# Routed experts in units of four, two and one blocks: 120, 16 and 20 of them where 85, 64 and 64 were

## The chip, the core and the metric

The kernel runs on one core of a Trainium2 chip. The metric is device time in microseconds (us) of one execution, the median of the runs shown. Engines are named as in the profile: PE (TensorE, with PEld for its weight loads), DVE (VectorE), ACT (ScalarE), POOL (GpSimd), SP (SyncE, which here only issues DMAs).

## What is computed

An input of 8 x 1024 rows of 512 goes through a modulated linear layer and then through a mixture of experts whose result is added to the input. Cut to what matters:

```python
y = clip(((x * styles) @ weight.T) * dcoefs + bias, -256, 256)   # per batch row
shared = silu(y @ sh_gate_w) * (y @ sh_up_w) @ sh_down_w          # hidden 1024
topk_idx, w = _route(y, router_w, e_bias)                         # 8 of 64 experts a row, by groups
order = argsort(topk_idx.reshape(-1), stable=True)                # rows sorted by expert
g, u = ragged_dot(sorted_x, gate_w, sizes), ragged_dot(sorted_x, up_w, sizes)   # hidden 256
o = ragged_dot(silu(g) * u, down_w, sizes) * weight_of_row
out = x + shared + zeros.at[tok].add(o)
```

There are 8192 x 8 = 65,536 pairs of a row and an expert. The expert biases are spread widely, so the lists of the experts are of very unequal length, from none to 8191 rows.

## The kernel before, in words

**Precision.** Every product is made of three matmuls in the fast fp32 form: the operand is split into a rounded part ("hi", written by ACT) and a rest ("lo", written by DVE), and hi x hi, hi x lo and lo x hi are summed in PSUM.

**Stages.** First the modulated layer writes its rows y to DRAM (L316 to L373). Then a shared stage of 16 x 8 = 128 steps computes the shared expert (L1100 to L1161). Beside it a generator, `route_slots` (L814), sorts the rows by expert: it is driven a little at a time from each step; its small matmuls (`later`) run in the next step, and each `HOP` ends its turn for one step. It writes 512 columns of (row, weight) to a DRAM table by indirect DMAs, five a step (L1031), reads the table back in groups of 128 blocks (L1000), holds it until step 119 (L1154), and turns it into `slot_tok` and `slot_w` (L1006). The last four steps also begin the first routed unit (`early`).

**Blocks and units.** A block is 128 rows of one expert. The number of blocks of an expert, in binary, gives its fours, at most one two and at most one one. The places of the blocks are numbered ones first, then twos, then fours, each aligned to its size. A static list of units (L777 to L787) covers these places: units of one, two and four blocks, with 4 x NU = 532 blocks. Since the places are aligned, a unit of one can also do a quarter of a four, or a half of a two. Which expert a unit belongs to is computed on the chip (`iexp`, L949). Fours beyond the 133 places of four go to tail units behind the list, groups of 8, 4, 2 and 1 under branches (L1173 to L1179).

**A unit** (`plan`, L608). Each block is gathered by an indirect DMA of POOL into `xg` (12 buffers, L534), turned by four PE transposes (L538) and split into `xh` and `xl` (two buffers, by the unit's parity). The expert's weights are loaded by SP (L531) into a raw buffer, `wg` for gate and up and `wd` for down; the load is skipped when the buffer already holds this expert. ACT and DVE split them (L549, L69) into `gh`, `gl`, `dh`, `dl` (two buffers, by parity), which for unit i may begin only when unit i-2 has ended its gate and up. There are three raw buffers: one for the ones, one for the fours, one for the twos.

Gate and up of a four or a two (`part`, L561) have the weights as the loaded operand and all rows of the unit as the moving one: 48 matmuls of 512 columns for a four, of 256 for a two. A one (`half`, L570) has the rows as the loaded operand and gate and up together as 512 moving columns: 12 matmuls, after which the hidden row block must be turned by two transposes (L575). The hidden rows are split too (`hh`, `hl`); `down_c` (L581) runs six matmuls of 512 columns for each block, ACT scales the result by the row's weight (L585), and POOL adds it into the output with an accumulating indirect DMA (L588). The first such DMA of a unit waits until all of the unit before have landed.

**The order of the work.** `plan` gives each task an engine, a duration, a delay, the tasks it depends on and a due time. `arrange` (L729) runs through them in model time: an engine that is free takes, of its tasks that are ready, the one due first. The order that comes out is the program order on PE, ACT, DVE, SP and POOL. `DOWN` and `TURN` (L605, L606) set by how much, for each size of unit, the downs come after the hidden rows and the turns ahead of gate and up (first number), and the distance from block to block (second number).

Of the kernel before, what the change touches and what calls it, by code (L numbers as in the profile page):

```python
# [13 lines left out]
I32 = mybir.dt.int32  # L14
# [7 lines left out]
P = 128  # L22
# [8 lines left out]
KC = C // P  # L31
HC = HS // P
QT = 512
NH = E
NP = E
NF = 85
NU = NF + NH // 4 + NP // 2
TBITS = 4
GROUPS = [(b, 1 << b) for b in range(TBITS - 1, -1, -1)]
NX = (1 << TBITS) - 1  # L40
NSB = (NU + NX) * 4
NE = NH + NP + NF + NX
NTRASH = 4 * P
# [20 lines left out]
def body(ctx, tc, xT, x, condT, wT, vecs, affT, rwT, ebias, wexp, shgu, shdn, cst, out):  # L64
# [28 lines left out]
    tbit = pp.tile([P, 8], I32, name="tbit")  # L93


    dctx = ExitStack()
# [401 lines left out]
    class Unit:  # L498


        def __init__(self, unit, block, nb, i):
# [100 lines left out]

    DOWN = {1: (-8.5, 1.0), 2: (0.0, 4.2), 4: (3.4, 5.4)}  # L605
    TURN = {1: (9.9, 1.0), 2: (1.4, 3.4), 4: (16.6, 0.0)}  # L606

    def plan(units):  # L608

# [14 lines left out]
        for n, u in enumerate(units):  # L624
# [6 lines left out]
                before = [T[lw, x, 2 if a else c] for x in ("wh", "wl") for c in ((0, 1) if a == 0 else (2,))] if lw is not None else []  # L631
                add((i, "load", a), "SP", 0.1, 12.0 if a == 0 else 8.0, due - 22 + 4 * a, lambda u=u, a=a: load(u, a), *before)
            for c in range(2):
                add((i, "wh", c), "ACT", 1.08, 0.15, due - 4.8 + 2.2 * c, lambda u=u, c=c: w_hi(u, c), T[i, "load", 0], get((i - 2, "gu")))
                add((i, "wl", c), "DVE", 1.22, 0.15, due - 3.7 + 2.2 * c, lambda u=u, c=c: w_lo(u, c), T[i, "wh", c], get((i - 2, "gu")))
            xlo = []
            for s in range(u.nb):
                g = ng
# [74 lines left out]
                    lo.append(l_)  # L713
                ddue = t0 + 2.5
            for c in (2,):
                add((i, "wh", c), "ACT", 1.08, 0.15, ddue - 2.4, lambda u=u, c=c: w_hi(u, c), T[i, "load", 1], *hq)
                add((i, "wl", c), "DVE", 1.22, 0.15, ddue - 1.2, lambda u=u, c=c: w_lo(u, c), T[i, "wh", c], *hq)
# [61 lines left out]
    for i in range(sum(want)):  # L779
        lag = [want[k] * (i + 1) / sum(want) - count[k] for k in range(3)]  # L780
        kind = 2 if i == 0 else max((k for k in range(3) if count[k] < want[k] and not (k == 0 and units[-1].nb == 1)), key=lambda k: lag[k])
        n = count[kind]
        count[kind] += 1
        units.append((
            lambda: Unit(n, n, 1, i), lambda: Unit(NH + n, NH + 2 * n, 2, i), lambda: Unit(NH + NP + n, NH + 2 * NP + 4 * n, 4, i),
        )[kind]())
    assert tuple(count) == want  # L787
    tasks, byname = plan(units)
    groups, r = [], 0
    for b, size in GROUPS:  # L790
        groups.append((b, [Unit(NH + NP + NF + r + q, 4 * (NU + r + q), 4, q) for q in range(size)]))
        r += size

    with ExitStack() as bctx:
# [19 lines left out]
        def route_slots():  # L814
# [102 lines left out]
            V.tensor_scalar(tbit[:, TBITS:TBITS + 1], ti[:, 5:6], 1, None, ALU.min)  # L917
# [11 lines left out]
            V.tensor_scalar(g2[:, :TBITS], gp[:E, :TBITS], 4.0, 4.0 * NU, ALU.mult, ALU.add)  # L929
            off = 0  # L930
            for b, n in GROUPS:
                V.tensor_scalar(ex[:, off:off + n], cs[:E, C_GRP:C_GRP + n], g2[:, b:b + 1], None, ALU.add)
                off += n
            yield 1.8

# [29 lines left out]
            for g in range(0, NSB, P):  # L965
                n = min(P, NSB - g)

                bk = sbt.tile([E, 2, P], F32, name="bk")
                V.tensor_scalar(bk[:, 0], block[:E], float(g), None, ALU.add)
                m0 = 4 * NU - g  # L970
                if m0 < n:
                    V.tensor_copy(bk[:, 0, m0:n].rearrange("e (u f) -> e u f", f=4), ex.unsqueeze(2).to_broadcast([E, NX, 4]))
# [12 lines left out]
                later.append(row)  # L985
                yield HOP
# [18 lines left out]
                    n = min(P, NSB - g * P)  # L1005
                    PE.transpose(ps[:, q * P:q * P + n], tg[g][:n].rearrange("b (s w) -> b w s", w=2)[:, w], ident[:n, :n])  # L1006

            whole = NSB // P
            for part in ([(g, 0) for g in range(whole)], [(g, 1) for g in range(whole)], [(whole, 0), (whole, 1)]):
                later.append(lambda part=part: turn(part))  # L1010
                yield HOP
                if part[0][0] == 0:
                    V.tensor_copy((slot_tok, slot_w)[part[0][1]][:, :whole * P], ps[:, :whole * P])
                else:
                    for w in range(2):
                        V.tensor_copy((slot_tok, slot_w)[w][:, whole * P:], ps[:, w * P:w * P + NSB - whole * P])
            yield 0


# [68 lines left out]
        with tc.manual_schedule(engines={ET.PE, ET.SP, ET.Activation, ET.DVE}):  # L1088
# [11 lines left out]
            for i, (j, c) in enumerate(steps):  # L1100
# [66 lines left out]
    with cctx:  # L1167
        allot(cctx.enter_context(tc.tile_pool(name="cp", bufs=1, reuse_waits="tile")), kinds, None)
        allot(cctx.enter_context(tc.tile_pool(name="psc", bufs=1, space=PSUM, reuse_waits="tile")), pkinds, None)
        with tc.manual_schedule(engines={ET.PE, ET.SP, ET.Activation, ET.DVE}):  # L1170
            for t in arrange(tasks, begun):
                t.do()
            with tc.If(nc.values_load(tbit[0:1, TBITS:TBITS + 1], min_val=0, max_val=1) > 0):  # L1173
                for b, tail in groups:
                    held.clear()
                    line[0] = None
# [46 lines left out]
```

## Time and profile before

| | |
|---|---|
| median of 3 runs | 3764.27 us (3763.72 to 3764.33) |
| the profiled execution itself | 3764.38 us |
| its span, first to last instruction | 3762.5 us |
| mean granted clock of PE over the span | 0.995 |
| PE / DVE / ACT / POOL busy | 99% / 59% / 50% / 57% |
| routed stage, 1325 to 3742 us: PE busy | 2415.56 of 2417.00 us |
| moved by DMA | 467.79 MB, mean 124 GB/s |

The modulated layer takes the first two to three fortieths of the span, the shared stage lasts until about 1325 us, and the rest is the routed stage. Two kinds of lines are used below. A piece of the chain is a stretch of the chain of work that ended last: start, length, engine, tile, line and count; its length is the distance to the next piece, so that it can be added up. A window gives, for a stretch of the span, its length, then for each engine its busy time and count, then the granted clock, the busy share of the DMA engines and what they moved in GB/s. The busy time of a single matmul overlaps that of the next and can't be added up.

### The profile page before, as it was taken

To read this page: it belongs to the slowest core of one execution; us is meant where nothing else is said; L and a number is where in the kernel's file an instruction comes from. 1 tells how busy PE (TensorE), PEld (TensorE's weight loads), DVE (VectorE), ACT (ScalarE), POOL (GpSimd) and SP (SyncE) were. 2 spreads that over 40 slices of the span, in tenths; PEclk is the share of its full clock that TensorE was granted. 3 is DMA by queue.
4 is the path that set the end of the run, shared out by engine and by line. 5 is a ranking of instruction groups with operands and counts; after the bars stand their busy time and mean duration, and the time that the engine had idled before them with its cause. 6 is when DMAs were issued, how large, how long until landed. Compare 5 with 4: busy or idle time off the path is not lost.

```text
span 3762.5 us, 53389 instructions
## 1 busy us (share of the span) xinstructions
PE 3721.5 (99%) x19047; PEld 3120.3 (83%) x19047; DVE 2206.0 (59%) x3376; ACT 1888.8 (50%) x2891; POOL 2127.6 (57%) x1596
## 2 busy tenths in 40 slices
PE   9999999999999999999999999999999999999998
PEld 7777888888888888888888888888888888888886
DVE  6766656666542265666556566556566656656654
ACT  5652112111111166666666566666566666666664
POOL 0003666666654066666666565566665666666663
PEclk9999999999999999999999999999999999999999
DMA  7762212222122277787777776766766766666664
GB/s 252 234 175 65 66 35 52 52 48 55 38 49 58 95 185 168 157 210 168 168 162 152 157 148 137 152 131 137 165 126 125 136 133 117 135 115 116 118 116 65
DMA packets 234392, 467.79 MB, mean 124 GB/s; under 512 B 42578, under 2 KB 75362, under 8 KB 228355
## 3 DMA queue, kind: packets, MB, share of 16 engines
q0 software_dynamic: 135792, 280.15, 40.5%
q1 hardware_dynamic: 97331, 183.06, 15.8%
q8 instruction: 152, 2.49, 0.3%
q14 instruction: 125, 1.02, 0.1%
q10 hardware_dynamic: 992, 1.06, 0.1%
HBM read 532.75 MB, written 195.63 MB: 194 GB/s over the span
## 4 chain that ended last, share of the span: by engine, by line
PE 95%; DVE 2%; DMA 1%; ACT 1%; issue 0%; SPq 0%; POOL 0%; DVEq 0%; POOLq 0%; ACTq 0%
PE pg L561 35%; PE po L581 20%; PE gu L121 18%; PE po L1061 9%; PE pg L570 5%; PE pt L538 4%; PE py L316 3%; DMA xr<-in_xT 1%; PE pg L575 0%; PE plt L341 0%; DVE yl L69 0%; DVE yt L353 0%; DVE xl L300 0%; ACT yf L322 0%; DMA yr<-yT_d 0%
## 5 line engine op out<-in xcount | busy, mean ns | idle before, releaser
L588 POOL DMA_INDIRECT out<-oc,tokw x532 | 955.0, 1795 | 563.6 <-ACT oc L585 250.0
L534 POOL DMA_INDIRECT xg<-y_d,tokw x532 | 595.4, 1119 | 440.8 <-PE pt L538 194.4
L1031 POOL DMA_INDIRECT tab_d<-tokw,ad x512 | 564.8, 1103 | 492.7 <-DVE h L133 205.8
L561 PE MATMUL pg<-xh,gh 128*128 128x512 f32 (+1 forms) x2384 | 834.1, 350 | 0.0
L561 PE MATMUL pg<-xh,gl 128*128 128x512 f32 (+1 forms) x2384 | 823.5, 345 | 0.0
L561 PE MATMUL pg<-xl,gh 128*128 128x512 f32 (+1 forms) x2384 | 820.8, 344 | 0.0
L69 DVE TENSOR_TENSOR gl<-wg,gh 128x1024 fp32r<-128x1024 f32 x426 | 519.6, 1222 | 108.1 <-ACT gh L549 96.9
L561 PEld LDWEIGHTS pg<-xh,gl 128*128 128x128 f32 x2384 | 449.8, 189 | 57.1
L561 PEld LDWEIGHTS pg<-xl,gh 128*128 128x128 f32 x2384 | 449.9, 189 | 55.7
L561 PEld LDWEIGHTS pg<-xh,gh 128*128 128x128 f32 x2384 | 449.8, 189 | 53.0
L549 ACT CAST gh<-wg 128x1024 fp32r<-128x1024 f32 x426 | 448.2, 1055 | 0.0
L585 ACT ACTIVATE oc<-po,tokw 128x512 f32<-128x512 f32 x532 | 369.5, 695 | 153.1 <-PE po L581 136.2
L69 DVE TENSOR_TENSOR xl<-pt,xh 128x512 fp32r<-128x512 f32 x532 | 356.4, 686 | 137.0 <-ACT xh L541 106.4
L581 PE MATMUL po<-dh,hh 128*128 128x512 f32 x1064 | 427.0, 401 | 1.0 <-ACT hh L710 1.0
L581 PE MATMUL po<-dh,hl 128*128 128x512 f32 x1064 | 418.4, 393 | 0.4 <-DVE hl L69 0.4
L581 PE MATMUL po<-dl,hh 128*128 128x512 f32 x1064 | 416.0, 391 | 0.0
L121 PE MATMUL gu<-yh,guh 128*128 128x512 f32 x1024 | 401.7, 392 | 3.1 <-ACT yh L72 3.1
L121 PE MATMUL gu<-yl,guh 128*128 128x512 f32 x1024 | 403.1, 394 | 0.2 <-DVE yl L69 0.2
L708 DVE TENSOR_TENSOR hf<-hf,pg 128x512 f32<-128x512 f32 x170 | 116.8, 687 | 483.6 <-PE pg L561 473.7
L121 PE MATMUL gu<-yh,gul 128*128 128x512 f32 x1024 | 400.2, 391 | 0.0
L541 ACT CAST xh<-pt 128x512 fp32r<-128x512 f32 x532 | 301.2, 587 | 177.2 <-PE pt L538 81.6
L69 DVE TENSOR_TENSOR dl<-wd,dh 128x1024 fp32r<-128x1024 f32 x213 | 260.4, 1223 | 89.5 <-ACT dh L549 69.5
(234 smaller groups left out, 5615.2 us busy)
## 6 DMA issues: line engine op xcount, KB each, us to landing
wg<-in_wexp SPq DMA_DIRECT2D x213, 1024.0 KB
wd<-in_wexp SPq DMA_DIRECT2D x213, 512.0 KB
y_d<-yt SPq DMA_DIRECT2D x64, 256.0 KB
xn<-in_x SPq DMA_DIRECT2D x64, 256.0 KB
out<-xn SPq DMA_DIRECT2D x64, 256.0 KB
xr<-in_xT SPq DMA_DIRECT2D x60, 256.0 KB
yT_d<-yf SPq DMA_DIRECT2D x60, 256.0 KB
yr<-yT_d SPq DMA_DIRECT2D x60, 256.0 KB
```

Of the source, the lines that this page charges most:

```text
L69: V.tensor_tensor(o, a, b, ALU.subtract)
L121: i_ = PE.matmul(p_, lhsT=w_[:, q * KC + k], rhs=y_[k], start=n == 0, stop=n == 3 * KC - 1)
L534: queued(GP.indirect_dma_start(xg[g % RXG].bitcast(F32), None, y_d, IOA(slot_tok[:, u.block + s:u.block + s + 1], 0)))
L541: S.copy(xh[u.xq][:, :, s * P:(s + 1) * P], pt_of(g).bitcast(F32))
L549: S.copy(a[u.q][:, sl], (wg, wg, wd)[c][u.kind][:, sl])
L561: PE.matmul(out, lhsT=w_[u.q][:, c:c + P], rhs=x_[u.xq][:, k, :w], start=n == 0, stop=n == 3 * KC - 1)
L570: PE.matmul(out.rearrange("p (o h) -> p o h", o=2), lhsT=x_[u.xq][:, k, :P], rhs=wv[:, k], start=n == 0 and i == 0, stop=n == 5 and i == 1)
L581: PE.matmul(po[d % 2], lhsT=h_[u.q][:, k, s * P:(s + 1) * P], rhs=w_[u.q][:, k * C:(k + 1) * C], start=n == 0, stop=n == 5)
L585: S.mul(oc[d % ROC], po[d % 2], slot_w[:, u.block + s:u.block + s + 1])
L588: i_ = queued(GP.indirect_dma_start(out, IOA(slot_tok[:, u.block + s:u.block + s + 1], 0), oc[d % ROC], None, compute_op=ALU.add))
L1031: i_ = GP.indirect_dma_start(places, IOA(ad, 0), tw, None)
L1061: PE.matmul(acc[j][s], lhsT=h_[:, ts], rhs=w_[c], start=c == 0 and n == 0, stop=c == HC - 1 and n == 2)
```

## The change

The static list keeps 133 places of four, but covers them by 120 fours, 16 twos and 20 ones. Since there are now fewer ones and twos than experts, a surplus has to be taken care of: experts beyond the twentieth with a single block have it rounded up to a two, and those beyond the sixteenth with a two have it rounded up to a four (two more matmuls and two more turns of the generator). The rounding can push more fours over the 133 places, so the tail grows from 15 to 47 units: five groups of eight and groups of four, two and one. The table of slots grows from 592 to 720 blocks, six groups of 128 for five.

The raw weights of the fours go to two buffers in turn, and ones and twos share the third. The due times of the turns, the downs and the splits of the weights are others.

```diff
-NH = E
-NP = E
-NF = 85
+NH = 20
+NP = 16
+NF = 120
 NU = NF + NH // 4 + NP // 2
-TBITS = 4
-GROUPS = [(b, 1 << b) for b in range(TBITS - 1, -1, -1)]
-NX = (1 << TBITS) - 1
+TBITS, TBIG = 3, 5
+GROUPS = [(TBITS + q, 8) for q in range(TBIG)] + [(b, 1 << b) for b in range(TBITS - 1, -1, -1)]
+NX = sum(n for _, n in GROUPS)
+TANY = TBITS + TBIG
...
-            self.kind = {1: 0, 4: 1, 2: 2}[nb]
+            self.kind = 2 if nb < 4 else n % 2
...
-    DOWN = {1: (-8.5, 1.0), 2: (0.0, 4.2), 4: (3.4, 5.4)}
-    TURN = {1: (9.9, 1.0), 2: (1.4, 3.4), 4: (16.6, 0.0)}
+    DOWN = {1: (-8.2, 1.0), 2: (6.6, 5.1), 4: (6.6, 5.1)}
+    TURN = {1: (9.9, 1.0), 2: (13.2, 1.9), 4: (18.0, -1.3)}
...
-                add((i, "wh", c), "ACT", 1.08, 0.15, due - 4.8 + 2.2 * c, ...
-                add((i, "wl", c), "DVE", 1.22, 0.15, due - 3.7 + 2.2 * c, ...
+                add((i, "wh", c), "ACT", 1.08, 0.15, due - 8.3 + 2.2 * c, ...
+                add((i, "wl", c), "DVE", 1.22, 0.15, due - 7.2 + 2.2 * c, ...
...
-                add((i, "wh", c), "ACT", 1.08, 0.15, ddue - 2.4, ...
-                add((i, "wl", c), "DVE", 1.22, 0.15, ddue - 1.2, ...
+                add((i, "wh", c), "ACT", 1.08, 0.15, ddue + 3.8, ...
+                add((i, "wl", c), "DVE", 1.22, 0.15, ddue + 5.0, ...
...
             V.tensor_scalar(eci[:, 0:1], eci[:, 0:1], 7, None, ALU.logical_shift_right)
+            for most, bit in ((NH, 0), (NP, 1)):
+                V.tensor_scalar(eci[:, 1:2], eci[:, 0:1], bit, 1, ALU.logical_shift_right, ALU.bitwise_and)
+                V.tensor_copy(ecnt[:, 1:2], eci[:, 1:2])
+                later.append(lambda: PE.matmul(ps[:E, 1:2], lhsT=cs[:E, C_CUM:C_CUM + E], rhs=ecnt[:, 1:2], start=True, stop=True))
+                yield HOP
+                V.tensor_scalar(ecnt[:, 2:3], ps[:E, 1:2], most + 0.5, float(1 << bit), ALU.is_gt, ALU.mult)
+                V.tensor_tensor(ecnt[:, 2:3], ecnt[:, 2:3], ecnt[:, 1:2], ALU.mult)
+                V.tensor_copy(ecnt[:, 3:4], eci[:, 0:1])
+                V.tensor_tensor(ecnt[:, 3:4], ecnt[:, 3:4], ecnt[:, 2:3], ALU.add)
+                V.tensor_copy(eci[:, 0:1], ecnt[:, 3:4])
...
-            whole = NSB // P
-            for part in ([(g, 0) for g in range(whole)], [(g, 1) for g in range(whole)], [(whole, 0), (whole, 1)]):
+            half_ = [(g, w) for w in range(2) for g in range(4, NG)]
+            for part in ([(g, 0) for g in range(4)], [(g, 1) for g in range(4)], half_):
...
-                    for u in [units[next(q for q in range(len(units)) if units[q].kind == k)] for k in (1, 0)]:
+                    for u in [units[next(q for q in range(len(units)) if units[q].kind == k)] for k in (0, 1)]:
```

The other edits fit the tail's bits, the experts of its units and the copies out of the table to the new sizes. With these numbers the static list begins F F 1 F F 2 F F F (F a four, 1 a one, 2 a two) where it began F 1 2 F 1 2 F 1 2, has 156 units for 213, and ends with F F for 2 F.

More of the change, by code (lines that the diff above doesn't have):

```diff
@@ L92, in body @@
     iexp = pp.tile([1, NE], I32, name="iexp")
-    tbit = pp.tile([P, 8], I32, name="tbit")
+    tbit = pp.tile([P, TANY + 1], I32, name="tbit")
     dctx = ExitStack()
@@ L498, in body, with __init__ @@
     class Unit:
-        def __init__(self, unit, block, nb, i):
+        def __init__(self, unit, block, nb, i, n):
             self.unit, self.block, self.nb, self.i = unit, block, nb, i
-            self.kind = {1: 0, 4: 1, 2: 2}[nb]
+            self.kind = 2 if nb < 4 else n % 2
             self.q, self.xq, self.e = i % 2, i % RX, None
@@ L633, in plan @@
             for c in range(2):
-                add((i, "wh", c), "ACT", 1.08, 0.15, due - 4.8 + 2.2 * c, lambda u=u, c=c: w_hi(u, c), T[i, "load", 0], get((i - 2, "gu")))
-                add((i, "wl", c), "DVE", 1.22, 0.15, due - 3.7 + 2.2 * c, lambda u=u, c=c: w_lo(u, c), T[i, "wh", c], get((i - 2, "gu")))
+                add((i, "wh", c), "ACT", 1.08, 0.15, due - 8.3 + 2.2 * c, lambda u=u, c=c: w_hi(u, c), T[i, "load", 0], get((i - 2, "gu")))
+                add((i, "wl", c), "DVE", 1.22, 0.15, due - 7.2 + 2.2 * c, lambda u=u, c=c: w_lo(u, c), T[i, "wh", c], get((i - 2, "gu")))
             xlo = []
@@ L715, in plan @@
             for c in (2,):
-                add((i, "wh", c), "ACT", 1.08, 0.15, ddue - 2.4, lambda u=u, c=c: w_hi(u, c), T[i, "load", 1], *hq)
-                add((i, "wl", c), "DVE", 1.22, 0.15, ddue - 1.2, lambda u=u, c=c: w_lo(u, c), T[i, "wh", c], *hq)
+                add((i, "wh", c), "ACT", 1.08, 0.15, ddue + 3.8, lambda u=u, c=c: w_hi(u, c), T[i, "load", 1], *hq)
+                add((i, "wl", c), "DVE", 1.22, 0.15, ddue + 5.0, lambda u=u, c=c: w_lo(u, c), T[i, "wh", c], *hq)
             chain = [T[units[n - 1].i, "out", s] for s in range(units[n - 1].nb)] if n else []
@@ L784, in body @@
         units.append((
-            lambda: Unit(n, n, 1, i), lambda: Unit(NH + n, NH + 2 * n, 2, i), lambda: Unit(NH + NP + n, NH + 2 * NP + 4 * n, 4, i),
+            lambda: Unit(n, n, 1, i, n), lambda: Unit(NH + n, NH + 2 * n, 2, i, n), lambda: Unit(NH + NP + n, NH + 2 * NP + 4 * n, 4, i, n),
         )[kind]())
@@ L790, in body @@
     for b, size in GROUPS:
-        groups.append((b, [Unit(NH + NP + NF + r + q, 4 * (NU + r + q), 4, q) for q in range(size)]))
+        groups.append((b, [Unit(NH + NP + NF + r + q, 4 * (NU + r + q), 4, q, q) for q in range(size)]))
         r += size
@@ L916, in route_slots @@
             yield 1.8
-            V.tensor_scalar(tbit[:, TBITS:TBITS + 1], ti[:, 5:6], 1, None, ALU.min)
+            V.tensor_scalar(tbit[:, TANY:TANY + 1], ti[:, 5:6], 1, None, ALU.min)
+            for q in range(TBIG):
+                V.tensor_scalar(tbit[:, TBITS + q:TBITS + q + 1], ti[:, 5:6], float(-8 * q - 7), 0.0, ALU.add, ALU.max)
+            V.tensor_scalar(tbit[:, TBITS:TANY], tbit[:, TBITS:TANY], 1, None, ALU.min)
             for b in range(TBITS - 1, -1, -1):
@@ L931, in route_slots @@
             for b, n in GROUPS:
-                V.tensor_scalar(ex[:, off:off + n], cs[:E, C_GRP:C_GRP + n], g2[:, b:b + 1], None, ALU.add)
+                V.tensor_scalar(ex[:, off:off + n], cs[:E, C_GRP:C_GRP + n], g2[:, b:b + 1] if b < TBITS else 4.0 * (NU + off), None, ALU.add)
                 off += n
@@ L969, in route_slots @@
                 V.tensor_scalar(bk[:, 0], block[:E], float(g), None, ALU.add)
-                m0 = 4 * NU - g
+                m0 = max(4 * NU - g, 0)
                 if m0 < n:
-                    V.tensor_copy(bk[:, 0, m0:n].rearrange("e (u f) -> e u f", f=4), ex.unsqueeze(2).to_broadcast([E, NX, 4]))
+                    x0, xn_ = (g + m0) // 4 - NU, (n - m0) // 4
+                    V.tensor_copy(bk[:, 0, m0:n].rearrange("e (u f) -> e u f", f=4), ex[:, x0:x0 + xn_].unsqueeze(2).to_broadcast([E, xn_, 4]))
                     V.tensor_tensor(bk[:, 0, m0:n], bk[:, 0, m0:n], four[:E, m0:n], ALU.add)
@@ L1006, in turn @@
                     PE.transpose(ps[:, q * P:q * P + n], tg[g][:n].rearrange("b (s w) -> b w s", w=2)[:, w], ident[:n, :n])
-            whole = NSB // P
-            for part in ([(g, 0) for g in range(whole)], [(g, 1) for g in range(whole)], [(whole, 0), (whole, 1)]):
+            half_ = [(g, w) for w in range(2) for g in range(4, NG)]
+            for part in ([(g, 0) for g in range(4)], [(g, 1) for g in range(4)], half_):
                 later.append(lambda part=part: turn(part))
                 yield HOP
-                if part[0][0] == 0:
-                    V.tensor_copy((slot_tok, slot_w)[part[0][1]][:, :whole * P], ps[:, :whole * P])
+                if part is not half_:
+                    V.tensor_copy((slot_tok, slot_w)[part[0][1]][:, :4 * P], ps)
                 else:
                     for w in range(2):
-                        V.tensor_copy((slot_tok, slot_w)[w][:, whole * P:], ps[:, w * P:w * P + NSB - whole * P])
+                        o = w * (NG - 4) * P
+                        V.tensor_copy((slot_tok, slot_w)[w][:, 4 * P:], ps[:, o:o + NSB - 4 * P])
             yield 0
@@ L1172, in body @@
                 t.do()
-            with tc.If(nc.values_load(tbit[0:1, TBITS:TBITS + 1], min_val=0, max_val=1) > 0):
+            with tc.If(nc.values_load(tbit[0:1, TANY:TANY + 1], min_val=0, max_val=1) > 0):
                 for b, tail in groups:
```

## The prediction

> **What bounds the kernel now.** I read the page from the top, then the chain that ended last by line, then the routed stage by itself. The page first: span, part 1, and part 4 with its shares by engine and by line.
>
> ```profile
> span 3762.5 us, 53389 instructions
> ...
> PE 3721.5 (99%) x19047; PEld 3120.3 (83%) x19047; DVE 2206.0 (59%) x3376; ACT 1888.8 (50%) x2891; POOL 2127.6 (57%) x1596
> ...
> PE 95%; DVE 2%; DMA 1%; ACT 1%; issue 0%; SPq 0%; POOL 0%; DVEq 0%; POOLq 0%; ACTq 0%
> PE pg L561 35%; PE po L581 20%; PE gu L121 18%; PE po L1061 9%; PE pg L570 5%; PE pt L538 4%; PE py L316 3%; DMA xr<-in_xT 1%; PE pg L575 0%; PE plt L341 0%; DVE yl L69 0%; DVE yt L353 0%; DVE xl L300 0%; ACT yf L322 0%; DMA yr<-yT_d 0%
> ```
>
> The reader is to see that 95% of the chain is PE itself, and that the routed units (L561, L581, L570, L538, L575) make about two thirds of it. But an average over stages proves nothing for one stage, so next come the windows (length, then busy time of PE, PEld, DVE, ACT and POOL with counts, clock, DMA share, GB/s) and PE's waits in the routed stage.
>
> ```profile
> 1580.25:1693.87 113.62, 113.62 (x630) 96.88 (x630) 68.19 (x84) 71.86 (x109) 74.41 (x51) 1.00 0.83 199
> 2098.58:2212.03 113.45, 113.45 (x631) 96.83 (x630) 67.71 (x84) 71.82 (x109) 66.69 (x49) 1.00 0.74 168
> ...
> 1325.00:3742.00 2417.00, 2415.56 (x13347) 2058.14 (x13347) 1445.48 (x1765) 1522.12 (x2291) 1529.94 (x1046) 1.00 0.70 143
> ```
>
> ```profile
> PE po L581 <- ACT hh L710: 1.0, 2, 0.8
> PE po L581 <- DVE hl L69: 0.4, 1, 0.4
> ```
>
> In 2417 us of the routed stage PE is idle for 1.4 us, at a granted clock of 1.00. DVE (60%), ACT (63%), POOL (63%) and the DMA engines (share 0.70) all have room. So the stage is as long as PE's list of instructions, and the change is worth what it takes out of that list, unless it opens waits. Work taken from ACT, DVE or the DMA queues is worth nothing by itself.
>
> **How much work there is.** From the reference's inputs, in double precision, 65,536 assignments fall on 28 experts' lists and fill 529 blocks: 123 fours, 10 twos, 17 ones. Before: 85 + 64/4 + 64/2 = 133 places of four; after: 120 + 20/4 + 16/2 = 133, 532 blocks both times. The lists need 133 in either kernel: 17 ones are below the limit of 20 and 10 twos below 16, so nothing is rounded up and the tail stays empty, with no place to spare. The trace agrees for before: L588 runs 532 times, no tail unit. PE then does 532 turns and 532 downs before and after; only the gate/up work is done in other shapes.
>
> **The price of the shapes.** These are pieces of the chain (start, length, line, count). A four's gate/up is 48 matmuls of 512 columns, a two's 48 of 256, a one's 12 of 512 at L570 and two transposes at L575.
>
> ```profile
> 1485.41 1.39 PE pg L570 x6
> ...
> 1488.48 1.48 PE pg L570 x6
> ...
> 1493.74 0.24 PE pg L575 x2
> 1493.98 1.43 PE pg L561 x12
> ...
> 1530.66 7.14 PE pg L561 x48
> ...
> 1544.38 11.04 PE pg L561 x48
> ```
>
> - The last piece is a four's 48, uninterrupted: 11.04 us, 2.76 a block (0.230 a matmul).
> - A two: one part of 12 took 1.43; the 7.14 are three such parts and one part of a four, (7.14 - 2.76) / 3 = 1.46 each. So a two costs 5.72 to 5.84, and half a four 5.52: 0.20 to 0.32 more. 48 twos go: 9.6 to 15.4 us.
> - A one: 2 x 1.39 + 0.24 = 3.02, or 1.39 + 1.48 + 0.24 = 3.11 with a slow start behind transposes; a quarter of a four is 2.76: 0.26 to 0.35 more. 44 ones go: 11.4 to 15.4 us.
>
> Together 21.0 to 30.8 us. I take 22, near the lower end: the excess of 1.48 over 1.39, and of 7.14, stands behind a group of transposes, and the 532 turns stay, so most of these restarts will only stand before another instruction.
>
> The Trainium skill, in "TensorE: Matmul & The Clock Gate", section "Back-to-back issue gap", gives the gap of isolated warm matmuls as N/2.4 + 2.5 ns, 109 ns at 256 columns and 216 at 512. By it a two would cost only 0.06 us more than half a four (an estimate), 48 of them 3 us, and the whole would come to about 3753. The trace shows 119 and 230 ns, a larger fixed part, so I don't go by it.
>
> **What is added to PE's list.** The rounding runs one small matmul for each of two limits, the table has six groups of slots for five (three more matmuls of L983, of 0.25 us each) and 12 transposes for 10 (0.28 each). Seven times some 0.2 us: 1.5 us, because PE is 35.00 of 35 us busy in the shared stage at 1270 to 1305. The bounds are 0 and 2. The added VectorE instructions, some 30 on a few columns, delay the table by perhaps three steps of the shared stage (8.2 us each). This lies beside two covers: the 512 table writes are paced and end at 1185, while the last L983 ran at 1101; and the fetched table (1194) waits until 1257 for its turn. If both covers were gone, the kernel could not start its first gathers in time; 84 + 63 us against some 25 say they hold.
>
> **What is moved, at no cost.** ACT loses 57 x 3 casts of 1.055 us, DVE 57 x 3 of 1.22: off the chain, worth nothing. POOL's queue keeps 532 gathers and 532 scatters. The first scatter of a unit waits until the unit before has landed, 213 times before and 156 after. Within fours POOL needs 4 x (1.80 + 0.30 + 1.12 + 0.30) = 14.1 of the four's 11.04 + 4 x (1.39 + 0.31) = 17.8 us; a landing wait of 4.3 on top would be 18.4, over the limit, if no gather filled it. Before, a four, a two and a one (31.9 us between the L575 pieces at 1461.80 and 1493.74) asked 24.6 + 3 x 4.3 = 37.5, more over the limit, and PE never waited: gathers do fill these waits.
>
> On SP's queue the skipped loads change. Following the experts along the units, 45 loads are made before and 60 after (each hot expert is now read into both buffers of the fours): 15 x 1.5 MB more, some 10 GB/s over the stage beside 143. The dense window above, 0.83 and 199 GB/s, kept PE full. The shortest distance between two uses of a raw buffer rises from 31.9 us (one to one) to 35.7 (two fours). Cost nothing; with that cover gone, each load would hold PE for the time of 1.57 MB, 7.9 us at the dense window's 199 GB/s (an estimate from that row).
>
> **The start.** The second unit becomes a four where it was a one. It wants more preparation, but over a four's 17.8 us of PE instead of a four's and a one's with a two close behind. I take 0, bounds -1 and +3; PE lost 3 us around 1308 to 1345 before.
>
> **The end.** POOL's rows at the end (start, length, what, idle before and who ended it):
>
> ```profile
> 3736.55 1.56 POOL L588 DMA_INDIRECT out<-oc,tokw  x1 [0.30 <-issue]
> 3742.39 1.55 POOL L588 DMA_INDIRECT out<-oc,tokw  x1 [4.27 <-DMA out<-oc,tokw]
> ```
>
> The last four's first scatter waits 4.27 us for the two before it. After, a four stands there, and with the new due times its last two downs come behind the last gate/up: they fill the 1.5 us that PE waits for the hidden rows, but their scatter lands later. PE's last down ended 17.8 us before the end (3744.7 to 3762.5); now the path is 0.75 (oc) + 1.6 + 4.3 + 4 x 1.87 behind the earlier unit's last down, plus the same 13: some 21.4 behind PE's last. 3.6 longer, 1.5 of idle saved: some +2.2, bounds 0 and +5.
>
> **Sum.** -22 + 1.5 + 2.2 = -18.3 us against the profiled execution's 3764.38 (span 3762.5, 1.9 around it), which is 0.1 above the median: 3746.
>
> **Rivals.**
> - A. Larger gain: the slow starts vanish with the shapes. Then 30.8 - 3.7 = 27 us, 3737. For it: they are 0.07 to 0.09 each in the rows; against: the turns stay.
> - B. The twos save nothing, a column costing the same in either width: 11.4 - 3.7 = 8 us, 3757. Against: 1.43 is over half of 2.76 in every row.
> - C. Slower: a wait before a four that follows a small unit. In F1F and F2F (36 places after, 14 before) the four's x and raw-weight splits may begin only when the four two places earlier has ended its gate/up, so DVE (four x rests at 0.69, two weight rests at 1.22, with the hidden work 7 to 8 us) has only the small unit and the downs beside it, 8 to 14 us. A stall of 0.8, the longest in this stage, at all 36 would be 29 us: 3775. It decides from 0.5 us a place (18.3 / 36). Against: seven F1F and seven F2F lie between about 2100 and 2900, as in the window 2098.58:2212.03, PE busy for all 113.45 us; and more downs are now held back to fill.
> - D. The change doesn't leave the tail empty: a count over its limit opens a tail four that is not overlapped, 17.8 us of PE and a second ending of some 24: 3788 or more. Against: the counts above; only the missing spare place speaks for it.
>
> **How the numbers follow.** Forecast 3746: 0.74. A: 0.07. B: 0.09. C: 0.08. D: 0.02. What a measurement of this kernel can tell from no change is about 0.2%, 7.5 us: below 3756.7 is faster (forecast and A, 0.81), B is the same (0.09), C and D slower (0.10). The range goes from A's side to B, 3736 to 3757, and leaves out C and D and a little around.
>
> **What would show it.** In the changed profile: PE idle in the routed stage still a few us at most; 5760 matmuls of 512 columns and 768 of 256 at L561's successor, 240 at L570's, 40 at L575's; the stage some 20 us shorter for 532 scatters. Right for the end: a landing wait before the last four's first scatter. Wrong: PE waiting for the splits of x or weights behind small units, for a raw-weight load, or a scatter count above 532.

## The result and the profile after

After the change the kernel takes 3730.81 us (median of 6 runs, 3729.29 to 3734.11), where before took 3764.35 beside it (6 runs, 3763.72 to 3766.98): 33.5 us less, a ratio of 0.991 with an interval of 0.9897 to 0.9923. The forecast was 3746 with a range that began at 3736. The sign was right; the gain is 1.8 times the one forecast, and the time lies below the range.

The profiled execution of after took 3734.11 us, the longest of the six. From its page, the span, part 1, a row of part 3 (queue: packets, MB, share) and a group of part 5:

```profile
span 3732.3 us, 49590 instructions
PE 3686.6 (99%) x17819; PEld 3051.5 (82%) x17819; DVE 2006.0 (54%) x3196; ACT 1736.3 (47%) x2676; POOL 2090.1 (56%) x1597
q1 hardware_dynamic: 101651, 206.63, 18.0%
L591 POOL DMA_INDIRECT out<-oc,tokw x532 | 915.6, 1721 | 662.4 <-ACT oc L588 197.8
```

The groups of after, each shape apart (line, tile, shape, count | busy, mean ns of one):

```profile
L564 PE MATMUL pg<-xh,gh 128*128 128x512 f32 x1920 | 764.2, 398 | 0.0
L564 PE MATMUL pg<-xh,gh 128*128 128x256 f32 x256 | 74.5, 291 | 0.0
L573 PE MATMUL pg<-gh,xh 128*128 128x512 f32 x80 | 31.7, 396 | 0.0
L578 PE MATMUL pg<-cs,hf 128*128 128x128 f32 x40 | 7.6, 271 | 0.0
```

Each row of L564 and L573 is one of three products, so there are 5760 matmuls of 512 columns, 768 of 256, and 240 in ones, with 40 transposes: the counts that the prediction named. There are 532 additions, so the tail did not run. The DMA queue of the weights moved 206.63 MB (183.06 before), the 15 added loads. The routed stage of after, as a window with the columns of the prediction:

```profile
1318.00:3708.00 2390.00, 2390.00 (x12117) 1992.16 (x12115) 1237.71 (x1550) 1370.81 (x2076) 1490.28 (x1047) 1.00 0.74 154
```

PE is busy for all 2390.00 us; the view of PE's waits in this stage is empty. DVE and ACT have lost 208 and 151 us, which are worth nothing by themselves. The DMA share rose from 0.70 to 0.74, and no transfer holds PE.

So far all is as forecast. Where the time went shows when the span is cut by PE's own instructions: the front up to the first matmul of the shared expert's gate and up (L121, L124 in after), the shared stage to its last down, the routed stage to the last routed down, and the end. All in us, from the traces:

| | front | shared | routed | shared + routed | end | span |
|---|---|---|---|---|---|---|
| before | 245.0 | 1081.0 | 2418.3 | 3499.3 | 18.1 | 3762.5 |
| after | 242.1 | 1076.5 | 2389.1 | 3465.6 | 24.6 | 3732.3 |
| difference | -2.9 | -4.5 | -29.2 | -33.7 | +6.4 | -30.2 |

These are the lengths of the profiled executions, and after's is the longest of its six; the end is counted from the start of the last down's last matmul. The front has no term in the prediction, and the other three differences are not what it has. The routed stage gave 29.2 for a forecast of 22 (and some 1.4 of idle). The shared stage, to which the change adds instructions (+1.5 forecast), became shorter by 4.5. And the end grew by 6.4 where 3.6 was worked out.

The shared stage is the thread to pull: the change touches none of its 36 matmuls a step, and PE's idle time there is the same, 6.95 us of 1080 before and 7.13 us of 1076 after.

### The profile page after: what moved, and what is told of

It is laid out like the page before. It is cut to its first block, busy times and chain, and to the rows that moved or that the text cites. A ratio compares the mean times of both kernels' runs of the same rounds, so it can differ in the third digit from the quotient of the medians.

```text
span 3732.3 us, 49590 instructions
## 1 busy us (share of the span) xinstructions
PE 3686.6 (99%) x17819; PEld 3051.5 (82%) x17819; DVE 2006.0 (54%) x3196; ACT 1736.3 (47%) x2676; POOL 2090.1 (56%) x1597
## 3 DMA queue, kind: packets, MB, share of 16 engines
q1 hardware_dynamic: 101651, 206.63, 18.0%
## 5 line engine op out<-in xcount | busy, mean ns | idle before, releaser
L591 POOL DMA_INDIRECT out<-oc,tokw x532 | 915.6, 1721 | 662.4 <-ACT oc L588 197.8
L564 PE MATMUL pg<-xh,gh 128*128 128x512 f32 (+1 forms) x2176 | 838.7, 385 | 0.0
L564 PE MATMUL pg<-xh,gl 128*128 128x512 f32 (+1 forms) x2176 | 823.5, 378 | 0.0
L564 PE MATMUL pg<-xl,gh 128*128 128x512 f32 (+1 forms) x2176 | 821.6, 378 | 0.0
L564 PEld LDWEIGHTS pg<-xh,gl 128*128 128x128 f32 x2176 | 409.1, 188 | 78.6
L564 PEld LDWEIGHTS pg<-xl,gh 128*128 128x128 f32 x2176 | 409.6, 188 | 71.7
L564 PEld LDWEIGHTS pg<-xh,gh 128*128 128x128 f32 x2176 | 408.8, 188 | 71.1
L711 DVE TENSOR_TENSOR hf<-hf,pg 128x512 f32<-128x512 f32 x240 | 164.9, 687 | 483.8 <-PE pg L564 458.6
L124 PE MATMUL gu<-yh,guh 128*128 128x512 f32 x1024 | 400.9, 391 | 3.4 <-ACT yh L75 3.4
L72 DVE TENSOR_TENSOR gl<-wg,gh 128x1024 fp32r<-128x1024 f32 x312 | 376.2, 1222 | 51.3 <-ACT gh L552 49.3
L124 PE MATMUL gu<-yl,guh 128*128 128x512 f32 x1024 | 401.3, 392 | 0.2 <-DVE yl L72 0.2
L124 PE MATMUL gu<-yh,gul 128*128 128x512 f32 x1024 | 398.8, 389 | 0.0
L552 ACT CAST gh<-wg 128x1024 fp32r<-128x1024 f32 x312 | 324.1, 1049 | 27.0 <-PE pg L564 23.4
L708 ACT ACTIVATE hf<-pg 128x512 f32<-128x512 f32 x240 | 144.0, 600 | 293.0 <-PE pg L564 279.3
```

The source lines that it names most:

```text
L72: V.tensor_tensor(o, a, b, ALU.subtract)
L124: i_ = PE.matmul(p_, lhsT=w_[:, q * KC + k], rhs=y_[k], start=n == 0, stop=n == 3 * KC - 1)
L552: S.copy(a[u.q][:, sl], (wg, wg, wd)[c][u.kind][:, sl])
L564: PE.matmul(out, lhsT=w_[u.q][:, c:c + P], rhs=x_[u.xq][:, k, :w], start=n == 0, stop=n == 3 * KC - 1)
L591: i_ = queued(GP.indirect_dma_start(out, IOA(slot_tok[:, u.block + s:u.block + s + 1], 0), oc[d % ROC], None, compute_op=ALU.add))
L708: si = add((i, "si", m), "ACT", 0.61, 0.15, due + 5.46 * m + 3.1, lambda b=b, f=f: S.activation(hf[f % 3], pg[b % 4], AF.Silu), p, *wait_h ...
```

## The experiments

Two theories stood against each other. **Shapes:** the fours are cheaper than the rows of before showed, and fewer slow starts remain (the prediction's rival A, extended). **Places:** the new sizes of four tables move other tiles in SBUF, and a matmul's price depends on where its operands lie. The tiles lie in two stacks, one from the low addresses and one from the high. In the low stack the change makes tokw 5760 bytes a partition for 4736, cs 2448 for 2676, iexp 812 for 912, tbit 36 for 32; rounded up to 32 that is +1024 - 224 - 96 + 32 = +736 bytes for all that lies behind them (`dh1`, `xh1`, `dnh7` among them). The high stack (`gh0`, `guh0`, `xh0`) stays. Beside these, smaller questions: the due times, the second raw buffer, the end.

The time and the stages of each run; "before" is the median of before on the same chip, the columns behind it are from the profiled execution:

| run | us | before | ratio, 95% interval | front | shared | routed | end |
|---|---|---|---|---|---|---|---|
| e1_before_moved | 3748.33 | 3764.42 | 0.9956 (0.994 to 0.9973) | 240.6 | 1073.8 | 2413.9 | 18.3 |
| e2_after_old_places | 3742.74 | 3764.42 | 0.9942 (0.9925 to 0.9959) | 245.4 | 1080.3 | 2392.2 | 22.2 |
| e3_after_old_dues | 3729.20 | 3764.42 | 0.9905 (0.9888 to 0.9921) | 244.4 | 1074.9 | 2387.2 | 24.2 |
| e4_before_new_dues | 3767.11 | 3764.42 | 1.0008 (0.9998 to 1.0017) | 245.7 | 1081.3 | 2417.4 | 23.7 |
| e5_before_moved_32 | 3753.83 | 3764.52 | 0.9972 (0.9963 to 0.9982) | 244.4 | 1079.5 | 2411.1 | 18.6 |
| e6_before_moved_768 | 3764.17 | 3764.52 | 0.9999 (0.9989 to 1.0008) | 242.7 | 1080.0 | 2418.3 | 18.4 |
| e7_fewer_ones | 3759.32 | 3764.52 | 0.9991 (0.9982 to 1.0001) | 241.1 | 1080.5 | 2408.7 | 24.4 |
| e8_fewer_twos | 3774.37 | 3764.52 | 1.0028 (1.0017 to 1.0038) | 242.4 | 1082.0 | 2427.3 | 19.5 |
| e9_one_buffer_for_fours | 3732.85 | 3763.74 | 0.9917 (0.99 to 0.9933) | 240.4 | 1076.2 | 2391.7 | 23.6 |
| e10_early_last_downs | 3730.08 | 3763.74 | 0.9909 (0.9892 to 0.9925) | 240.1 | 1076.2 | 2390.5 | 22.0 |
| e11_old_dues_early_last | 3728.27 | 3763.74 | 0.9904 (0.9888 to 0.9921) | 241.3 | 1074.8 | 2388.4 | 21.7 |
| e12_after_moved_32 | 3747.56 | 3763.74 | 0.9957 (0.994 to 0.9974) | 248.0 | 1082.0 | 2392.2 | 22.9 |
| e13_before_right_moved | 3755.96 | 3764.88 | 0.9976 (0.9967 to 0.9986) | 242.4 | 1078.6 | 2411.5 | 18.6 |
| e14_after_right_moved | 3741.34 | 3764.88 | 0.9937 (0.992 to 0.9953) | 241.4 | 1081.9 | 2394.1 | 22.6 |

The front varies from 240.1 to 248.0 us between kernels that do the same there, so the sum of the shared and the routed stage is the cleaner measure of PE's prices.

### The places alone, in the kernel before

```diff
+    moved = pp.tile([P, 736], mybir.dt.uint8, name="moved")
+    V.memset(moved, 0.0)
```

Behind the table `tbit`, in before: nothing but the place of the low tiles changes.

> The kernel before with an unused tile of 736 bytes per partition put behind tbit: every tile of the left side of SBUF then lies 736 bytes higher, as in the changed kernel, and no instruction of the three stages is another. Theory A (place): the matmuls that stayed the same in the changed kernel got cheaper because their tiles lie elsewhere; then the shared stage goes from 1081.0 to about 1076.5 us and the routed stage falls by up to 7, together -4 to -11 us, 3753 to 3760. Rival B (company): they got cheaper because ACT and DVE make fewer casts beside them; then the shared stage and the routed stage stay within 2 us and the time is 3762 to 3767.

Measured: 3748.33, 16.1 us faster, more than theory A's 4 to 11, without one instruction of the work being another. The shared stage is 7.2 us shorter, the routed one 4.4; the rest lies in the front, and what made it shorter no run separates. The chain of before in the shared stage, and a four's gate and up in the routed stage (start, length, line, count):

```profile
716.76 5.60 PE gu L121 x24
722.36 2.77 PE po L1061 x12
725.13 5.60 PE gu L121 x24
...
741.85 5.44 PE gu L121 x24
...
1544.38 11.04 PE pg L561 x48
```

The same two views of e1:

```profile
717.04 5.49 PE gu L123 x24
722.54 2.72 PE po L1063 x12
725.25 5.50 PE gu L123 x24
...
733.47 5.44 PE gu L123 x24
...
1532.30 10.95 PE pg L563 x48
```

The same 24 matmuls take 5.49 for 5.60 us, the 12 behind them 2.72 for 2.77, the same four 10.95 for 11.04. These pieces are whole groups without a wait; it is the price of the single matmul that fell, by 2 to 5 ns. In the shared stage this holds for three of every eight steps: their gate and up weights (`guh0` to `guh2`, `gul0` to `gul2`) lie in the high stack, the tiles that are multiplied with them in the low one. In the other steps all of these tiles lie in the low stack, and their 24 matmuls take 5.44 us in both. Some 48 steps with 0.11 and 0.05 us are 7.7 us, about the 7.2 that the stage gave.

If the place decides, the size of the move should matter and not that something was moved. Two more sizes:

```diff
-    moved = pp.tile([P, 736], mybir.dt.uint8, name="moved")
+    moved = pp.tile([P, 32], mybir.dt.uint8, name="moved")
```

> The kernel before with a filler of 32 bytes where the first experiment had 736; no instruction of the three stages differs. A move of 736 gave -16 us (front 240.6, shared 1073.8, routed 2413.9). Theory: what counts is the start of a tile within 64 bytes: before, the tiles of the left side start at multiples of 64, after a move of 736 or 32 they start 32 off, as the tiles of the right side do (gh0, xh0, xl0 at 196576, 212960, 221152). Then 32 gives the same -16: 3746 to 3751. Rival: it is the distance, the larger place of the left side against something else (banks, neighbours); then 32 bytes give less than 5 us: 3759 to 3766.

> The kernel before with a filler of 768 bytes, a multiple of 64 (and of 256). Theory (start within 64 bytes): no gain, 3761 to 3767, shared stage about 1081 us. Rival (distance): 768 is about as far as 736, so about -16 us: 3746 to 3752.

32 bytes gave 10.7 us, 768 bytes nothing: 3764.17 for 3764.52. In e6 the routed stage is 2418.3 us, as in before, and the pieces have their old lengths again:

```profile
721.87 5.60 PE gu L123 x24
727.47 2.77 PE po L1063 x12
730.23 5.60 PE gu L123 x24
...
1541.16 11.04 PE pg L563 x48
```

So it is neither the added instruction nor that something was moved, but where the tiles come to lie. As 768 is a multiple of 64, of 128 and of 256, these runs do not say at which distance the price repeats.

The 32 bytes met neither forecast: not the 16 us of the theory, by which only the starts within 64 bytes count (there 32 and 736 are alike), and not the rival's less than 5. They also act elsewhere: the shared stage is only 1.5 us shorter, the routed one 7.2. The same pieces of e5's shared stage stay near those of before:

```profile
724.05 5.59 PE gu L123 x24
729.64 2.74 PE po L1063 x12
```

Is it the low tile's own address, or its relation to the tiles of the high stack? In e13 (before) and e14 (after) the high tiles are moved down by 32 bytes, by a filler at the end of two pools of that stack, and the low ones stay:

```diff
+        if hc == 2:
+            V.memset(sw.tile([P, 32], mybir.dt.uint8, name="moved"), 0.0)
...
+                    V.memset(c0.tile([P, 32], mybir.dt.uint8, name="moved2"), 0.0)
```

> The kernel before with the tiles of the right side (gh0, gl0, xh0, xl0, the first three gate and up weights of the shared stage) 32 bytes lower and the left side where it was; no instruction of the three stages differs. Theory: only the difference of the starts of the moving tile and of the next loaded tile counts. It is then the same, within 256 bytes, as in the run with the left side 32 bytes higher: 3752 to 3756, routed stage about 2411 us. Rival: the place of the left side counts by itself, then nothing changes: 3762 to 3767.

> The changed kernel with the right side 32 bytes lower, the left side as in the changed kernel. Theory (difference): the same difference as in the changed kernel with the left side 32 bytes higher, and as before: the gain of the place is lost, 3744 to 3750. Rival (place of the left side by itself): no change, 3729 to 3734.

Shared and routed together: e13 3490.1 us, e5 3490.6, for 3499.3 in before. Moving the high tiles down is worth what moving the low ones up is worth: the relation of the two stacks counts. In after the same 32 bytes cost: 3476.0 for 3465.6, and the time goes back to 3741.34, somewhat less than the forecast's 3744.

Sorted by the stacks in which the operands of three neighbouring 512-column matmuls lie, the mean distances from start to start are (ns, distances over 300 left out):

| operands | before | e1, +736 | e5, +32 | e6, +768 |
|---|---|---|---|---|
| shared stage, moving tiles low, weights high | 233.6 | 229.0 | 232.4 | 233.5 |
| shared stage, all low | 227.2 | 226.9 | 227.0 | 227.2 |
| routed stage, all high | 230.5 | 229.3 | 228.7 | 230.5 |
| routed stage, all low | 229.3 | 229.2 | 228.2 | 229.3 |

In e6 every row is back within 0.1 ns. In the shared stage the fall of e1 stands in the first row, 1033 distances with 4.5 ns each, 4.7 of the 7.2 us. In the routed stage matmuls with all operands in one stack became cheaper too, though the move leaves these operands to each other as they were. There the relation between neighbouring matmuls can't be the whole cause; what else counts was not separated.

Two single pairs, each a moving tile and the tile that is loaded for the next matmul, one in each stack (ns):

| moving, then loaded | before | e1, +736 | e5, +32 | e13, high -32 | e6, +768 |
|---|---|---|---|---|---|
| `dnh7`, `guh1` | 236.6 | 225.9 | 232.5 | 232.5 | 236.7 |
| `xh1`, `gh0` | 236.7 | 225.8 | 232.5 | 232.6 | 236.6 |

e5 and e13, with the same relation, agree. But the theory that only the starts within 64 bytes count fails on these rows: by it the pair is alike in e1 and in e5, and it takes 225.9 and 232.5. On average the 64 bytes do point the right way: over nine of these kernels and some 111,000 pairs, the second matmul starts 228.7 ns behind the first where the two starts are alike within 64 bytes and 233.3 where they are 32 bytes apart. That accounts for only some 6% of the spread. So the runs show that the place sets the price, and by how much in these kernels; the rule, and what in the chip makes it, they don't settle.

The Trainium skill, in "SBUF — State Buffer", section "Operand start alignment", says that an operand may start at any multiple of its element size, and that this concerns legality and not speed. All places here are legal in that sense; the runs add that they are not equal in price.

### The change at the old places

The counterpart: the whole change, with the low tiles where before had them. In e2 the tail is cut to 15 units (it does not run in either kernel), and a filler brings the rest to the very addresses of before; e12 keeps the kernel after whole and adds 32 bytes, 768 in all.

```diff
-TBITS, TBIG = 3, 5
+TBITS, TBIG = 3, 1
...
+    moved = pp.tile([P, 448], mybir.dt.uint8, name="moved")
+    V.memset(moved, 0.0)
```

> The changed kernel with a tail of 15 units instead of 47 (it is not run) and a filler tile, so that the tiles of the left side lie exactly where they lay before; five groups of slots instead of six. Theory A (place): the shared stage goes back up from 1076.5 to about 1080 us and the routed stage rises by up to 7: 3734 to 3742. Rival B (company): the routed stage stays at 2389 us within 2, the time at 3729 to 3733, and the shared stage's 4 us are then place alone or chance.

```diff
+    moved = pp.tile([P, 32], mybir.dt.uint8, name="moved")
+    V.memset(moved, 0.0)
```

> The changed kernel with a filler of 32 bytes, nothing else: the tiles of the left side then start at multiples of 64 as they did before, the right side's stay 32 off. Theory (what counts is whether the moving tile of a matmul and the next one's loaded tile start alike within 64 bytes): it loses most of what the place gave, 7 to 12 us: 3738 to 3743. Rival: the place gave its gain by something else, 32 bytes change less than 3 us: 3728 to 3734.

Measured: 3742.74 and 3747.56, 21.7 and 16.2 us faster than before, around the forecast of 18.3. Both lie above the bounds given for them, e12 by 4.6 us; e12 has the longest front of all runs (248.0). Their routed stages are the same, 2392.2 us, 26.1 below before's. The first and last starts of one product of the shared expert (count: duration, first to last start; shape) in after, and the same in e12:

```profile
L124 PE MATMUL gu<-yh,guh x1024: 387/389/796, 242.1 to 1310.5; 128*128 128x512 f32 x171
```

```profile
L126 PE MATMUL gu<-yh,guh x1024: 389/389/710, 248.0 to 1321.9; 128*128 128x512 f32 x171
```

From first to last it is 1068.4 us in after and 1073.9 in e12, for the same instructions; before has 1072.8 (245.0 to 1317.8).

Taking the distance from each matmul's start to the next, the sums over the routed stage can be set beside the terms of the forecast (us):

| kind | before | e2 | difference |
|---|---|---|---|
| fours (L561) | 945.0, 4080 x 0.2316 | 1332.4, 5760 x 0.2313 | |
| twos (L561) | 372.0, 3072 x 0.1211 | 93.7, 768 x 0.1220 | |
| ones and their transposes (L570, L575) | 192.0 | 58.1 | |
| all gate and up | 1509.0 | 1484.2 | -24.8 |
| turns | 163.0 | 162.2 | -0.8 |
| downs | 746.2 | 745.5 | -0.7 |

A two costs 48 x 0.1211 - 24 x 0.2316 = 0.255 more than half a four, 48 of them 12.2; a one 12 x 0.2368 + 2 x 0.0788 - 12 x 0.2316 = 0.22 more than a quarter, 44 of them 9.7. That is 21.9, of the 22 taken; the other 2.9 come from the ones that remain (0.2307 a matmul for 0.2368) and the fours.

### The due times

e3 is after with the due times of before, e4 before with those of after.

```diff
-    DOWN = {1: (-8.2, 1.0), 2: (6.6, 5.1), 4: (6.6, 5.1)}
-    TURN = {1: (9.9, 1.0), 2: (13.2, 1.9), 4: (18.0, -1.3)}
+    DOWN = {1: (-8.5, 1.0), 2: (0.0, 4.2), 4: (3.4, 5.4)}
+    TURN = {1: (9.9, 1.0), 2: (1.4, 3.4), 4: (16.6, 0.0)}
```

(and the four due times of the weight splits likewise.)

> The changed kernel with the due times of before (turns, downs, weight splits). Theory: PE's list is the same and the order finds work for PE either way, so PE idles less than 3 us in the routed stage; only the end changes, from 24.6 us behind the last down to some 20, because the last downs of the unit before the last come earlier: 3726 to 3733. Rival: the old due times, made for a mix with many small units, leave waits for x or weights before fours; 156 units with 0.3 us each would be 47 us: 3760 or more, seen as idle time of PE in the routed stage.

> The kernel before with the new due times alone (units, raw buffers and places as before). Theory: the due times are worth nothing to PE's list, the routed stage stays within 3 us of 2418: 3761 to 3768. Rival: the 7 us by which the unchanged matmuls of the routed stage got cheaper come from the order (fewer restarts behind transposes, other neighbours), then it falls by some 5 to 9 us: 3755 to 3760. A third way: the new due times starve PE in the old mix, 3770 or more.

Measured: 3729.20 with the old ones, 1.6 us below after, with overlapping spreads; and 2.7 us more in before with the new ones. In e4's profiled execution, 5.7 us longer than before's, nearly all of it lies in the end (23.7 for 18.1). In e3 the end did not shrink to some 20 as expected: it is 24.2. So either part of the change, the new mix or the new due times, lengthens the end by itself. The new due times give nothing here.

### One part of the mix at a time

e7 has 20 ones, 64 twos and 96 fours; e8 has 64 ones, 16 twos and 109 fours. Both are made from after, with the low tiles at before's addresses.

```diff
-NP = 16
-NF = 120
+NP = 64
+NF = 96
-TBITS, TBIG = 3, 5
+TBITS, TBIG = 3, 1
...
+    moved = pp.tile([P, 256], mybir.dt.uint8, name="moved")
```

> The changed kernel with 20 ones, 64 twos and 96 fours, a tail of 15 units that is not run, and a filler that puts the left side where it lay before. Only ones become fours: 44 of them at 0.22 to 0.35 us, the routed stage 9.7 to 15.4 us below 2418.3: 2403 to 2409; with an end some 4 us longer the time is about 3753 to 3759. Rival: what the whole change gave at the old places (26 us in the routed stage) comes from the twos, then the stage stays above 2412.

```diff
-NH = 20
-NF = 120
+NH = 64
+NF = 109
-TBITS, TBIG = 3, 5
+TBITS, TBIG = 3, 1
...
+    moved = pp.tile([P, 192], mybir.dt.uint8, name="moved")
```

> The changed kernel with 64 ones, 16 twos and 109 fours, otherwise as the run before. Only twos become fours: 48 of them at 0.20 to 0.32 us, the routed stage 9.6 to 15.4 us below 2418.3: 2403 to 2409; time about 3753 to 3759. The two parts together should give the 26 us of the routed stage; if they give less, the rest comes from the two changes together, fewer small units that interrupt the fours. Rival: twos save nothing (a column costs the same in either width), the stage stays above 2415.

The ones alone: routed stage -9.6, the 9.7 of the shapes; 6.3 of it goes back in the end (24.4), as with the new due times in e4. The twos alone, which should give 12.2, lose 9.0. The window 1330 to 3740 of e8, and PE's waits in it (waiting tile <- what ended it: us, times, longest):

```profile
1330.00:3740.00 2410.00, 2401.39 (x12149) 1993.77 (x12147) 1343.45 (x1684) 1450.94 (x2211) 1523.49 (x1042) 1.00 0.74 159
```

```profile
PE pt L543 <- DVE xl L72: 8.5, 16, 4.3
```

PE is idle for 8.6 us in this window where before has 1.4, and its turns wait for DVE's rests of x (`xl`), which read the tile that the turns write. One of the 16 waits, of 4.3 us, stands at the beginning of the stage (1341 us). The other 15, of some 0.3 us, stand where the blocks of a four are turned beside a one. Behind the window, at 3742 us, PE waits 3.3 us more, for the splits of `wd`. Behind both long waits the granted clock is low (0.54 from 1341 to 1347 us, 0.53 from 3743 to 3750), and matmuls of 512 columns start 0.427 us apart there.

Of its starts in the stage 42 come over 0.32 us behind the one ahead, 19.7 us beyond 0.235 each (before: 10 starts, 2.8 us; after: none): 6.4 us at the beginning, 6.6 at the end, 6.7 in between. With 12.2 saved and 16.9 more of stalls, the sum would be +4.7; +9.0 was measured, and the other 4 are not explained. In e8 a four follows a small unit between two fours in 78 places, in after in 36. So the prediction's rival C describes a wait that exists, at 15 of e8's 78 places, but it is a third of e8's stalls; in the change's own mix it costs nothing.

The parts do not add up: -9.6 and +9.0 against -26.1 together.

### The second raw buffer

```diff
-            self.kind = 2 if nb < 4 else n % 2
+            self.kind = {1: 0, 4: 1, 2: 2}[nb]
```

(and the order of the two early loads likewise.)

> The changed kernel with the raw weight buffers of before: one for the fours, one for the ones, one for the twos. Theory: the second buffer of the fours hides nothing that PE waits for, because most fours skip their load; only where the expert changes between two neighbouring fours can PE wait, some 15 places at a few us if at all: 3729 to 3740. Rival: two fours in a row need the second buffer; the load of 1.57 MB (7.9 us at 199 GB/s) behind the split of the unit before shows at each of the 15 changes, 60 us or more in all: above 3780, with PE waiting for the split of gate and up weights.

Measured: 3732.85, 2.0 us above after, with overlapping spreads. PE's waits in e9's routed stage, the same columns:

```profile
PE pg L564 <- DVE gl L72: 1.3, 1, 1.3
PE pg L564 <- ACT gh L552: 0.2, 1, 0.2
```

Two waits, of 1.3 and 0.2 us: two fours in a row leave enough time even with a single buffer.

### The end

POOL's rows at the end of after (start, length, what, idle before and who ended it):

```profile
3704.16 1.56 POOL L591 DMA_INDIRECT out<-oc,tokw  x1 [0.30 <-issue]
3712.12 1.58 POOL L591 DMA_INDIRECT out<-oc,tokw  x1 [6.40 <-ACTq L1193]
...
3717.75 1.56 POOL L591 DMA_INDIRECT out<-oc,tokw  x1 [0.30 <-issue]
```

The last unit's first addition waits 6.40 us for the unit before to land; before had 4.27. The row names ACT's queue, but the weighed rows of that addition were ready at 3704.74 us, before POOL came free at 3705.72, so of what it needs only the landing was still open. e10 gives the downs of the unit before last an early due time, so that its additions should have landed in time; e11 is e10 with the due times of before.

```diff
-ddue + DOWN[u.nb][0] + DOWN[u.nb][1] * s
+ddue + (DOWN[u.nb][0] + DOWN[u.nb][1] * s if n != len(units) - 2 or len(units) < 100 else -9.0 + 1.4 * s)
```

> The changed kernel; only the downs of the unit before the last get an earlier due time, so that they and their additions to the output come before the last unit's gate and up end. Theory: the last four's first addition then finds the earlier ones landed; the end falls from 24.6 us behind PE's last down to some 18 to 20, PE idles up to 1.5 us for the hidden rows: 3725 to 3729 beside 3730 for the change. Rival: POOL's four additions in a row set the end anyway, no gain: within 1 us of the changed kernel.

> The same edit in the changed kernel with the due times of before, which by itself took 3729.2: 3724 to 3727, below both kernels, if the two gains add up.

POOL's end of e10:

```profile
3701.70 1.56 POOL L591 DMA_INDIRECT out<-oc,tokw  x1 [0.30 <-issue]
3708.67 1.58 POOL L591 DMA_INDIRECT out<-oc,tokw  x1 [5.40 <-ACT oc L588]
```

The end became 22.0 for 24.6, and the time 3730.08, within the spread of after. The wait is still there: the unit before begins its own additions only when the one before it has landed, so an earlier down does not bring its last addition forward enough. The cure that was expected did not come. e11, 3728.27, is the lowest time of all and 2.5 us below after, with overlapping spreads; the 3724 to 3727 that the two gains together should have given did not come.

## Why the prediction was wrong

**The step that failed** is in its first part: "the stage is as long as PE's list of instructions, and the change is worth what it takes out of that list, unless it opens waits." The first half held: PE idles for 0 of 2390 us. The second silently takes the instructions that stay at their old price. They did not keep it: the change resizes four tables, the table of slots above all, that shifts the low tiles by 736 bytes, and many of the matmuls that stay became cheaper, by 1 to 11 ns each. e1, which has the shift alone, shows 16.1 us, 11.6 of it in the shared and the routed stage; e2, e12 and e14, which have the change with the stacks standing to each other as in before, are 10.5 to 16.8 above after, 6.9 to 10.4 of it in these stages. That moves the time from inside the range to below it. Nothing in the diff speaks of it but the size of the table of slots, and no term of the sum, no rival and no bound stood for it.

**Shapes: right.** 21.9 by the measured distances for 22, and 24.8 with what the remaining units gain. A two's 0.255 us lies inside its 0.20 to 0.32; a one's 0.22 lies below its 0.26 to 0.35. Rival A's mechanism did not come: there are 387 slow starts behind transposes in after for 380 in before, as the prediction argued, and the 2.9 us beyond 21.9 are no vanished starts. The result lies nearer to A's 3737 than to the forecast, but that is chance.

**Twos save nothing (B): wrong, as argued.** 0.1211 us for 256 columns against 0.2316 for 512. The estimate by the Trainium skill's "TensorE: Matmul & The Clock Gate", "Back-to-back issue gap" (3 us for the 48 twos) was too small as well: the runs give 12.2.

**Added work, +1.5: right as far as it can be seen.** In e12 and e14, whose stacks stand to each other as in before, the shared stage is 1.0 and 0.9 us longer (1082.0 and 1081.9 for 1081.0).

**SP's loads, no cost: right.** 15 more loads, 23.6 MB, and no wait of PE.

**Start, 0 (-1 to +3): not separable.** The second unit opens no wait at 1318; the front's own variation is larger than the bounds.

**End, +3.6 behind PE's last down: too low.** 4.1 and 4.8 at the old places, 6.4 in the profiled execution of after. The form was right, the landing wait before the last four's first addition; its length was taken from one row (4.27), and it measured 4.53 in e2, 5.40 in e10 and 6.40 in after. This error goes the other way than the miss.

**C, waits before a four behind a small unit:** no loss here, a part of e8's. **D, the tail:** did not run, 532 additions.

At the old places the errors of size are small: -26.1 in the routed stage, +4.1 at the end and -0.7 in the shared stage are -22.7 in e2, against -18.3. The forecast met the kernel that the change would have been without its shift, within 2 to 5 us (e12 3747.56, e2 3742.74, e14 3741.34 for 3746), and missed the kernel that it is.

## What to carry to other kernels

Where one engine is busy for the whole span, an edit that resizes a resident table can also move the operands of the instructions that stay, as it did here; look in a stage that the change does not touch, and if it became shorter or longer with the same idle time, the prices moved and not the work. Before crediting a rewrite with a gain below one per cent here, run the old kernel with a filler of the same size, and the new one at the old places. A part of a mix measured alone (e8) can lose what it gives together with the others.

## What the runs showed of the hardware

- The distance of two neighbouring 512-column matmuls depends on where their operands lie: the pair `dnh7`, `guh1` took 236.6, 232.5 or 225.9 ns with the low stack in place, 32 or 736 bytes higher, and 236.7 with 768. These moves were worth 10.7, 16.1 and 0.4 us of 3764. Moving the high stack down by 32 bytes gave the same 232.5. Most of the spread between pairs is left unexplained.
- Behind a group of PE transposes the first 512-column matmul is followed by the next only after some 0.30 us, for 0.23 within a stream. In after 387 groups of transposes are followed by such a slow start (256-column ones included), for 380 in before.
- After PE had waited 4.3 us in e8, the granted clock was 0.54 from 1341 to 1347 us, and eight 512-column matmuls started 0.427 us apart.
- The wait of one accumulating indirect DMA for the landing of the unit before took 4.27 to 6.40 us at the end of these kernels.
